# Two head groups in five score units in place of six, in a decoder layer with two attentions

## The chip, the cores and the metric

One core of a Trainium2 chip runs the kernel. The metric is the device time of one execution in microseconds, here 825.18 us as the median of three runs (825.09 to 825.27). Nothing is divided over cores; one core does all four batches.

## What is computed

A pre-norm decoder layer in float32, for 4 batches of 512 rows of 512 numbers, with 16 heads of 32:

```
x = x + self_attention(layernorm(x))        # q, k, v, o projections with biases, causal softmax
x = x + cross_attention(layernorm(x), ctx)  # ctx is both k and v, no projections;
                                            # causal, masked scores are -10000, not -inf
n = layernorm(x)
x = x + relu(n @ W_up.T) @ W_down.T + sum(softmax(top2(n @ W_gate.T))) * (n @ W_expert)
```

In both attentions a softmax over 512 keys is taken for each of 512 queries, 16 heads and 4 batches.

## The kernel before, in words

**Tiling.** The 512 rows of a batch are NT = 4 blocks of P = 128. The 16 heads are NC = 4 groups of HG = 4; one group fills the 128 partitions, a head in 32 of them. Scores are products over the 32 numbers of a head, so four heads' products run as four 32-row tiles of TensorE at once (lines L280 and L370). Values are products of 128 rows with 32 columns, four heads side by side (L429). All the projections are full 128 x 128 products of 512 columns (L221, L233, L638). PSUM is one pool of four `pair`s, each of 128 x 2 x 512 numbers in two banks; everything that TensorE writes takes a pair.

**Two passes over the scores.** An attention first finds the maximum of every row of scores (`maxima`, L267), and then computes the scores again, transposed, subtracts the maxima and takes the exponential (`scores`, L360).

- `maxima(g, blocks)` makes the scores of query blocks of group g against the keys up to the diagonal: blocks (0, 1) together, 128 + 256 = 384 columns, block 2 with 384, block 3 with 512. The four heads fill two pairs. ACT copies each to SBUF (L292, tiles `s`, tags pt0 to pt2 with two buffers each), POOL masks the diagonal (L298), and DVE's jobs reduce each block to its maxima (L310). After block 3 DVE splits the maxima into three bf16 parts (`split`, L323 to L332). `rows(g)` (L334) transposes these parts on TensorE (L338), and a copy makes them the rows `mrow`.
- `scores(g, blocks)` makes the scores of key blocks (0), (1) and (2, 3): 512, 384 and 256 + 128 columns. A bf16 product adds the rows of `mrow` to them (L381). ACT takes the exponentials (L402), POOL zeroes the upper part of the diagonal blocks (L404). `values(g, blocks, pts)` (L416) multiplies with v into the pair `pv`, and with a tile of ones for the denominators. For groups 0 to 2 of the self attention (`added`) the second product is left out: DVE adds the exponentials up over the key blocks (`add_up`, L453, row L458), and four products with ones, in the next group's first values, sum over the partitions (`summed`, L462). `inverse` (L481) transposes denominators and takes reciprocals on DVE; `scale` multiplies on POOL, `divide` on DVE.
- In the cross attention `masked` (L348) and `behind` (L623) add what the fully masked part contributes, since masked scores count as -10000.

**Order.** The order of TensorE, DVE, ACT and POOL is the program's, by hand; only the DMA queue is left to a scheduler. Each engine does its instructions in that order, and waits at its head.

`with_maxima(steps, a, first, norms)` (L780) interleaves the 12 units of an attention's maxima with `fill`: the matmuls of projections or of the feed-forward part of another batch, one of 512 columns at a time (a piece), spread over the units by a cost of their widths. The DVE jobs of one unit run in the fill of the next unit; a norm's job goes with each second unit; so `split(g - 1)` is in the fill of unit (g, blocks (0, 1)), and `rows(g - 1)` come two units later, in the fill of unit (g, block 3); rows(3) is left for the attend. The fill is 36 pieces in batch 0's self attention (`skip` 3 steps were run ahead of it), 34 in batches 1 and 2, 16 in batch 3; for the cross attention 20, 36, 20 and 25.

`attend(a, late)` (L810) runs the 12 units of scores, each followed by the values of the unit two before:

```
for n, (g, j) in enumerate(units):
    waiting.append((g, j, a.scores(g, j)))
    if n == 4:
        for copy in a.rows(late):
            copy(nc.scalar.copy)
    if len(waiting) > 2:
        values()
```

**The start of the cross maxima.** The normed rows of x are transposed (tp_q, L249) in two halves, and ACT copies each half to `cqT` (L257): blocks 0 and 1, then blocks 2 and 3. The first unit of the cross maxima, group 0 and blocks (0, 1), reads the first half only.

Of the kernel before, what the change touches and what calls it, by code (L numbers as in the profile page):

```python
# [18 lines left out]
P = 128  # L19
# [7 lines left out]
def decoder_layer(  # L27
# [232 lines left out]
    class Attention:  # L260
# [6 lines left out]
        def maxima(self, g, blocks):  # L267

            if blocks[0] == 0:
                self.nm[g] = small.tile([P, NT, HG], F32, tag="nm", name=f"nm_{self.name}_{g}")
            first = blocks[0]
            scs = [pair(f"sm_{self.name}_{g}_{first}_{n}") for n in range(2)]
            at = {i: sum((k + 1) * P for k in blocks if k < i) for i in blocks}
            N = sum((i + 1) * P for i in blocks)
            for i in blocks:
                for r in range(HG):
                    h = slice(r * HD, (r + 1) * HD)
                    nc.tensor.matmul(  # L280
                        scs[r // 2][:, r % 2, at[i] : at[i] + (i + 1) * P],
                        lhsT=self.q_t[h, g, i * P : (i + 1) * P],
                        rhs=self.k_t[h, g, : (i + 1) * P],
                        start=(i == first),
                        stop=True,
                        skip_group_check=(i != first),
                    )
            made = []
            for n in range(2):
                W, tag = {0: (S, "pt0"), 2: (N, "pt1"), 3: (S, "pt2")}[first]  # L290
                s = work.tile([P, 2, W], F32, tag=tag, name=f"s_{self.name}_{g}_{first}_{n}")
                nc.scalar.copy(s[:, :, :N], scs[n][:, :, :N])  # L292
                if len(blocks) > 1:

                    diagonal = s.rearrange("p u (k q) -> p (u k) q", k=2)[:, :, :P]
                else:
                    diagonal = s[:, :, N - P : N]
                nc.gpsimd.affine_select(  # L298
                    out=diagonal,
                    in_=diagonal,  # L300
                    compare_op=ALU.is_ge,
                    fill=NEG,
                    base=0,
                    pattern=[[0, 2 * len(blocks)], [-1, P]],
                    channel_multiplier=1,
                )
                made.append(s)

            def largest(n, i):
                nc.vector.tensor_reduce(  # L310
                    self.nm[g][:, i, 2 * n : 2 * n + 2],
                    made[n][:, :, at[i] : at[i] + (i + 1) * P],
                    axis=AX.X,
                    op=ALU.max,
                    negate=True,
                )

            jobs = [(lambda n=n, i=i: largest(n, i)) for n in range(2) for i in blocks]
            if blocks[-1] == NT - 1:
                jobs.append(lambda: self.split(g))  # L320
            return jobs
# [38 lines left out]
        def scores(self, g, blocks):  # L360


            at = {j: sum(S - k * P for k in blocks if k < j) for j in blocks}
            N = sum(S - j * P for j in blocks)
            name = f"{self.name}_{g}_{blocks[0]}"
            scs = [pair(f"sc_{name}_{n}") for n in range(2)]
            for j in blocks:
                for r in range(HG):
                    h = slice(r * HD, (r + 1) * HD)
                    nc.tensor.matmul(  # L370
                        scs[r // 2][:, r % 2, at[j] : at[j] + S - j * P],
                        lhsT=self.k_t[h, g, j * P : (j + 1) * P],
                        rhs=self.q_t[h, g, j * P :],
                        start=(j == blocks[0]),
                        stop=False,
                        skip_group_check=(len(blocks) > 1),
                    )
            for j in blocks:
                for r in range(HG):
                    h = slice(r * HD, (r + 1) * HD)  # L380
                    nc.tensor.matmul(  # L381
                        scs[r // 2][:, r % 2, at[j] : at[j] + S - j * P],
                        lhsT=onesb[h, :],
                        rhs=self.mrow[g][h, j * P :],
                        start=False,
                        stop=True,
                        skip_group_check=(len(blocks) > 1),
                    )
            pts = []
            if blocks[0] == 0 and g in self.added:  # L390

                self.sums[g] = act.tile(
                    [P, 2, 2, S], F32, tag=("ck_t", "beh_t")[g % 2], name=f"sum_{name}"
                )
            for n in range(2):

                W = N if len(blocks) == 1 else S
                if blocks[0] == 0 and g in self.added:
                    pt = self.sums[g][:, n]
                else:  # L400
                    pt = work.tile([P, 2, W], F32, tag=f"pt{blocks[0]}", name=f"pt_{name}_{n}")
                nc.scalar.activation(pt[:, :, :N], scs[n][:, :, :N], AF.Exp)  # L402
                diagonal = pt.rearrange("p u (k q) -> p (u k) q", k=len(blocks))[:, :, :P]
                nc.gpsimd.affine_select(  # L404
                    out=diagonal,
                    in_=diagonal,
                    compare_op=ALU.is_ge,
                    fill=0.0,
                    base=0,
                    pattern=[[0, 2 * len(blocks)], [1, P]],  # L410
                    channel_multiplier=-1,
                )
                pts.append(pt)
            return pts

        def values(self, g, blocks, pts):  # L416
# [3 lines left out]
            first, last = blocks[0] == 0, blocks[-1] == NT - 1  # L420
# [3 lines left out]
            at = {j: sum(S - k * P for k in blocks if k < j) for j in blocks}  # L424
            for u in range(1 if g in self.added else 2):
                for j in blocks:
                    for r in range(HG):
                        h = g * HG + r
                        nc.tensor.matmul(  # L429
                            pv[r * HD : (r + 1) * HD, u, j * P :],  # L430
                            lhsT=ones if u else self.v[:, j, h * HD : (h + 1) * HD],
                            rhs=pts[r // 2][:, r % 2, at[j] : at[j] + S - j * P],
                            start=(j == 0),
                            stop=(j == NT - 1),
                        )
# [5 lines left out]
            if first and g - 2 in self.added:  # L441
                self.scale(g - 2)
            if blocks == (1,) and g - 1 in self.added and g not in self.added:
# [9 lines left out]
        def add_up(self, g, blocks, pts):  # L453
            at = {j: sum(S - k * P for k in blocks if k < j) for j in blocks}
            for n in range(2):
                for j in blocks:
                    to = self.sums[g][:, n, :, j * P :]
                    nc.vector.tensor_tensor(  # L458
                        to, to, pts[n][:, :, at[j] : at[j] + S - j * P], ALU.add
                    )  # L460
# [319 lines left out]
    def with_maxima(steps, a, first=0, norms=()):  # L780
# [6 lines left out]
        units = [(g, i) for g in range(NC) for i in ((0, 1), (2,), (3,))]  # L787
        cost = [sum(k + 1.5 for k in i) for _, i in units]
        done, due, jobs = 0, 0.0, []
        for n, (g, i) in enumerate(units):  # L790
            new = a.maxima(g, i)
            if norms and n % 2 == 0:
                new.append(norms.pop(0))
            due += total * cost[n] / sum(cost)

            for k in range(round(due) - done):
                next(fill, None)
                done += 1
                if k == 1 and i[-1] == NT - 1 and g > 0:
                    jobs = a.rows(g - 1) + jobs  # L800
# [4 lines left out]
        for _ in fill:  # L805
            pass
        run(jobs)
        return NC - 1

    def attend(a, late):  # L810

        units = [(g, j) for g in range(NC) for j in ((0,), (1,), (2, 3))]
        waiting = []

        def values():
            g, j, pts = waiting.pop(0)
            a.values(g, j, pts)
            if g in a.added and j != (2, 3):
                a.add_up(*waiting[0])

        for n, (g, j) in enumerate(units):
            waiting.append((g, j, a.scores(g, j)))
            if n == 4:
                for copy in a.rows(late):
# [3 lines left out]
            if a.cross and j == (0,):  # L828
                behind(a.e, g)
            if a.cross and j == (2, 3):  # L830
                a.masked(g)
# [3 lines left out]
    with tc.manual_schedule(engines=BY_HAND):  # L835
# [7 lines left out]
        skip, between_cross, ahead = 3, [], []  # L843
# [100 lines left out]
```

## Time and profile before

| | us |
|---|---|
| median of three runs | 825.18 |
| the profiled execution | 825.04 |
| its span, first to last instruction | 823.3 |
| self attention, maxima, batch 0 / batch 3 (first score to first score of the attend) | 45.3 / 28.4 |
| self attention, attend, batch 0 | 31.1 |
| cross attention, maxima, batch 0 / batch 1 | 31.8 / 45.3 |
| cross attention, attend, batch 0 | 34.8 |

The stages are read from the timeline of the profiled execution, from the first instruction named to the first of the next stage; those of the maxima hold the fill too. The page gives each engine's busy time and share of the span: PE is TensorE's matmuls, PEld its weight loads, DVE, ACT and POOL the vector, scalar and GpSimd engines. The granted clock of TensorE was 1.00 through the span. The part of the page on the chain follows the work that ended last back from the end; its shares say which engine's work set the time. A group row gives line, engine, operation, output and input shapes and their number, then busy us and the mean in ns of one, then the idle time of that engine ahead of them and what ended it. In a timeline a row has start, duration, engine, line, operation, the number of neighbours put together, and the wait ahead of it in brackets.

### The profile page before, as it was taken

The numbers are of one execution on the slowest core, as the hardware profiler recorded it, in microseconds if no ns is written. First come the engines' busy times: TensorE is split into PE (matmuls) and PEld (weight loads), VectorE is DVE, ScalarE is ACT, GpSimd is POOL, SyncE is SP. The second block draws the span as 40 slices with busy tenths as digits, with TensorE's granted clock in tenths as the row PEclk, the third lists the DMA queues.
The fourth block names the chain that finished last, engine by engine and source line by source line (L and its number), as shares of the span: only waits on it lengthen the run. The fifth ranks groups of instructions, "written<-read, shape, count | busy, mean of one in ns | idle before, by whom it ended". The sixth has DMA issues, their size and how long they took to land.

```text
span 823.3 us, 14456 instructions
## 1 busy us (share of the span) xinstructions
PE 813.3 (99%) x5800; PEld 368.8 (45%) x5800; DVE 544.6 (66%) x937; ACT 398.0 (48%) x502; POOL 298.3 (36%) x549
## 2 busy tenths in 40 slices
PE   8999999999999999999999999999999999999998
PEld 7344454444444454334534445444543444444543
DVE  2578735967678834587868873596779835887512
ACT  2456526762456515556155652676257814565110
POOL 4434512343334732224233471244234643343100
PEclk9999999999999999999999999999999999999999
DMA  9600000001010000030100000000102000000101
GB/s 340 236 27 15 1 1 1 2 2 52 1 39 14 2 1 1 0 103 2 52 14 14 1 2 0 1 2 2 53 3 74 29 1 0 1 2 2 52 0 51
DMA packets 13539, 24.54 MB, mean 30 GB/s; under 512 B 1952, under 2 KB 1952, under 8 KB 13472
## 3 DMA queue, kind: packets, MB, share of 16 engines
q1 hardware_dynamic: 13184, 23.09, 8.3%
q8 instruction: 45, 0.74, 0.4%
q10 hardware_dynamic: 288, 0.52, 0.2%
q14 instruction: 22, 0.18, 0.1%
HBM read 19.42 MB, written 4.19 MB: 29 GB/s over the span
## 4 chain that ended last, share of the span: by engine, by line
PE 94%; DVE 3%; ACT 1%; issue 1%; DMA 0%; POOL 0%; ACTq 0%
PE pm_qk L233 13%; PE pv_c L429 9%; PE pm_d L221 7%; PE pm_u L233 7%; PE pm_v L221 7%; PE pm_o L638 7%; PE pm_e L221 6%; PE pv_s L429 6%; PE sm_c L280 6%; PE sc_s L370 6%; PE sc_c L370 5%; PE sm_s L280 5%; DVE nm_s L310 1%; PE sc_s L381 1%; PE sc_c L381 1%; PE tp_x L666 1%
## 5 line engine op out<-in xcount | busy, mean ns | idle before, releaser
L310 DVE TENSOR_REDUCE nm_c<-s_c 128x2 f32<-128x256 f32 (+3 forms) x128 | 96.3, 810 | 36.6 <-POOL s_c L298 36.6
L310 DVE TENSOR_REDUCE nm_s<-s_s 128x2 f32<-128x256 f32 (+3 forms) x128 | 96.7, 810 | 24.4 <-POOL s_s L298 24.4
L292 ACT COPY s_s<-sm_s 128x768 f32<-128x768 f32 (+1 forms) x96 | 78.8, 874 | 69.0 <-PE sm_s L280 51.2
L292 ACT COPY s_c<-sm_c 128x768 f32<-128x768 f32 (+1 forms) x96 | 78.9, 875 | 48.7 <-PE sm_c L280 34.1
L402 ACT ACTIVATE pt_c<-sc_c 128x768 f32<-128x768 f32 (+1 forms) x96 | 78.5, 884 | 29.3 <-PE sc_c L381 24.8
L298 POOL TENSOR_SCALAR_AFFINE_SELECT s_c<-s_c 128x256 f32<-128x256 f32 (+1 forms) x96 | 46.5, 485 | 118.5 <-ACT s_c L292 117.4
L404 POOL TENSOR_SCALAR_AFFINE_SELECT pt_c<-pt_c 128x256 f32<-128x256 f32 (+1 forms) x96 | 57.4, 605 | 70.5 <-ACT pt_c L402 69.5
L298 POOL TENSOR_SCALAR_AFFINE_SELECT s_s<-s_s 128x256 f32<-128x256 f32 (+1 forms) x96 | 46.6, 488 | 91.4 <-ACT s_s L292 90.6
L458 DVE TENSOR_TENSOR sum_s<-sum_s,pt_s 128x512 f32<-128x512 f32 (+1 forms) x72 | 63.1, 914 | 7.6 <-PE pv_s L429 6.6
L221 PE MATMUL pm_d<-wdown_sb,hT 128*128 128x512 f32 x128 | 61.7, 611 | 0.0
L221 PE MATMUL pm_e<-wexp_sb,fT 128*128 128x512 f32 x128 | 61.2, 608 | 0.4 <-DVE x L760 0.4
L233 PE MATMUL pm_u<-fT,wup_sb 128*128 128x512 f32 x128 | 60.6, 609 | 0.0
L402 ACT ACTIVATE pt_s<-sc_s 128x768 f32<-128x768 f32 (+1 forms) x72 | 55.8, 837 | 9.4 <-PE sc_s L381 7.0
L370 PE MATMUL sc_s<-qT,kT 32*128 32x128 f32 (+3 forms) x512 | 57.4, 466 | 1.9 <-DVE x L760 1.3
L233 PE MATMUL pm_qk<-xnT,wk_sb 128*128 128x512 f32 x120 | 59.3, 612 | 0.0
L221 PE MATMUL pm_v<-wv_sb,xnT 128*128 128x512 f32 x128 | 58.8, 600 | 0.0
L638 PE MATMUL pm_o<-wo_sb,oT_s 128*128 128x512 f32 x128 | 57.8, 596 | 0.0
L233 PE MATMUL pm_qk<-xnT,wq_sb 128*128 128x512 f32 x120 | 57.6, 606 | 0.0
L404 POOL TENSOR_SCALAR_AFFINE_SELECT pt_s<-pt_s 128x256 f32<-128x256 f32 (+1 forms) x72 | 48.4, 676 | 21.4 <-ACT pt_s L402 20.0
L370 PE MATMUL sc_c<-cqT,ckT 32*128 32x128 f32 (+3 forms) x512 | 51.5, 467 | 1.3 <-ACT pt_c L402 1.3
L280 PE MATMUL sm_c<-ckT,cqT 32*128 32x512 f32 (+3 forms) x512 | 49.4, 468 | 0.0
L280 PE MATMUL sm_s<-kT,qT 32*128 32x512 f32 (+3 forms) x512 | 48.1, 467 | 0.0
(148 smaller groups left out, 1183.5 us busy)
## 6 DMA issues: line engine op xcount, KB each, us to landing
cv<-in_ctx_dram SPq DMA_DIRECT2D x16, 256.0 KB, 4.2
out_dram<-x SPq DMA_DIRECT2D x16, 256.0 KB, 2.0
x<-in_x_dram SPq DMA_DIRECT2D x14, 256.0 KB, 4.1
xin<-in_x_dram SPq DMA_DIRECT2D x12, 256.0 KB, 2.6
wq_sb<-in_wq_dram SPq DMA_DIRECT2D x2, 512.0 KB, 6.0
wk_sb<-in_wk_dram SPq DMA_DIRECT2D x2, 512.0 KB, 7.7
wv_sb<-in_wv_dram SPq DMA_DIRECT2D x1, 1024.0 KB, 8.3
wo_sb<-in_wo_dram SPq DMA_DIRECT2D x1, 1024.0 KB, 9.9
```

Of the source, the lines that this page charges most:

```text
L221: nc.tensor.matmul(pm, lhsT=lhs_t[:, c, t * P : (t + 1) * P], rhs=w[:, c, :], start=(c == 0), stop=(c == NC - 1),)
L233: nc.tensor.matmul(pm, lhsT=w[:, c, f * P : (f + 1) * P], rhs=rhs_t[:, c, :], start=(c == 0), stop=(c == NC - 1),)
L280: nc.tensor.matmul(scs[r // 2][:, r % 2, at[i] : at[i] + (i + 1) * P], lhsT=self.q_t[h, g, i * P : (i + 1) * P], rhs=self.k_t[h, g, : (i + ...
L292: nc.scalar.copy(s[:, :, :N], scs[n][:, :, :N])
L298: nc.gpsimd.affine_select(out=diagonal, in_=diagonal, compare_op=ALU.is_ge, fill=NEG, base=0, pattern=[[0, 2 * len(blocks)], [-1, P]], cha ...
L310: nc.vector.tensor_reduce(self.nm[g][:, i, 2 * n : 2 * n + 2], made[n][:, :, at[i] : at[i] + (i + 1) * P], axis=AX.X, op=ALU.max, negate=True,
L370: nc.tensor.matmul(scs[r // 2][:, r % 2, at[j] : at[j] + S - j * P], lhsT=self.k_t[h, g, j * P : (j + 1) * P], rhs=self.q_t[h, g, j * P :] ...
L402: nc.scalar.activation(pt[:, :, :N], scs[n][:, :, :N], AF.Exp)
L404: nc.gpsimd.affine_select(out=diagonal, in_=diagonal, compare_op=ALU.is_ge, fill=0.0, base=0, pattern=[[0, 2 * len(blocks)], [1, P]], chan ...
L429: nc.tensor.matmul(pv[r * HD : (r + 1) * HD, u, j * P :], lhsT=ones if u else self.v[:, j, h * HD : (h + 1) * HD], rhs=pts[r // 2][:, r % ...
L458: nc.vector.tensor_tensor(to, to, pts[n][:, :, at[j] : at[j] + S - j * P], ALU.add)
L638: nc.tensor.matmul(pms[t // 2][:, t % 2, :], lhsT=a.out[:, c, t * P : (t + 1) * P], rhs=wo_sb[:, c, :], start=(c == 0), stop=(c == NC - 1),)
```

## The change

Both passes take two groups of heads in five units of 512 columns in place of six units of 384, 384 and 512:

- maxima of groups g and g + 1: [(g, 2), (g, 0)], [(g+1, 2), (g+1, 0)], [(g, 1), (g+1, 1)], [(g, 3)], [(g+1, 3)], where (g, i) is query block i of group g, widths 384 + 128, 256 + 256 and 512;
- attend: [(g, 0)], [(g, 3), (g, 1)], [(g, 2), (g+1, 2)], [(g+1, 0)], [(g+1, 3), (g+1, 1)], where (g, j) is key block j.

An attention has 10 units of each kind, not 12. Matmuls and their columns stay the same in number. Copies and exponentials are all of 128 x 1024, 80 of each in each kind of attention where there were 96. All of `s` and `pt` share one tag of six buffers of 128 x 2 x 512.

In `with_maxima` the fill is spread evenly; a norm's job goes with every unit; rows(0) and rows(1) come in the fill of units 5 and 6, and rows(2) and rows(3) in the attend, behind the scores of units 1 and 4 (`late`), with their copies on ACT. `skip` is 4, so batch 0's self maxima have 32 pieces of fill.

The unit [(g, 2), (g+1, 2)] ends nothing of group g but its values, and opens the `pv` of group g + 1 by its block 2: two `pv` pairs are alive then. `add_up` of (g+1, 2) is held until the values of (g+1, 0) are issued.

```diff
-            if norms and n % 2 == 0:
+            if norms:
                 new.append(norms.pop(0))
-            due += total * cost[n] / sum(cost)
-
-            for k in range(round(due) - done):
+            due += total / len(units)
+
+            count = round(due) - done
+            for k in range(count):
                 next(fill, None)
                 done += 1
-                if k == 1 and i[-1] == NT - 1 and g > 0:
-                    jobs = a.rows(g - 1) + jobs
+                if k == min(1, count - 1) and n in (5, 6):
+                    jobs = a.rows(n - 5) + jobs
                 run(jobs[:1])
                 jobs = jobs[1:]
...
-        return NC - 1
+        return late
...
-        units = [(g, j) for g in range(NC) for j in ((0,), (1,), (2, 3))]
-        waiting = []
+
+        units = []
+        for g in range(0, NC, 2):
+            units += [[(g, 0)], [(g, 3), (g, 1)], [(g, 2), (g + 1, 2)]]
+            units += [[(g + 1, 0)], [(g + 1, 3), (g + 1, 1)]]
+        waiting, held = [], []
 
         def values():
-            g, j, pts = waiting.pop(0)
-            a.values(g, j, pts)
-            if g in a.added and j != (2, 3):
-                a.add_up(*waiting[0])
-
-        for n, (g, j) in enumerate(units):
-            waiting.append((g, j, a.scores(g, j)))
-            if n == 4:
-                for copy in a.rows(late):
+            made = waiting.pop(0)
+            a.values(made)
+
+            if len(made) > 1 and made[0][1] == 2:
+                held.append(made[1:])
+            elif waiting and waiting[0][0][1] > 0:
+                if made[0][1] == 0 and held:
+                    a.add_up(held.pop())
+                a.add_up(waiting[0] if waiting[0][0][1] == 3 else waiting[0][:1])
+
+        for n, pieces in enumerate(units):
+            waiting.append(a.scores(pieces))
+            if n in late:
+                for copy in a.rows(late[n]):
                     copy(nc.scalar.copy)
             if len(waiting) > 2:
                 values()
-            if a.cross and j == (0,):
-                behind(a.e, g)
-            if a.cross and j == (2, 3):
-                a.masked(g)
+            if a.cross and pieces[0][1] == 0:
+                behind(a.e, pieces[0][0])
+            if a.cross and n % 5 in (2, 4):
+                a.masked(pieces[0][0])
...
-        skip, between_cross, ahead = 3, [], []
+        skip, between_cross, ahead = 4, [], []
```

`maxima`, `scores`, `values` and `add_up` take a list of pieces (g, block), each with its own columns, in place of one group and its blocks; `values` calls a new function `shares(g, blocks)` for each group of the unit:

```diff
+        def values(self, made):
+            for g in sorted({g for g, *_ in made}):
+                self.shares(g, [(j, c, pts) for k, j, c, pts in made if k == g])
+        def shares(self, g, blocks):
+            js = {j for j, *_ in blocks}
+            first = js == {0} if g % 2 == 0 else js == {2}
+            last = js == {2} if g % 2 == 0 else 1 in js
             if first:
                 self.pv[g] = pair(f"pv_{self.name}_{g}")
```

## The prediction

> **What bounds the kernel now.** I read the shares of busy time first, then the chain of waits, then the list of waits, and last the timeline of TensorE around the units that the change touches.
>
> ```profile
> PE 813.3 (99%) x5800; PEld 368.8 (45%) x5800; DVE 544.6 (66%) x937; ACT 398.0 (48%) x502; POOL 298.3 (36%) x549
> PE 94%; DVE 3%; ACT 1%; issue 1%; DMA 0%; POOL 0%; ACTq 0%
> ```
>
> TensorE is the bound nearly everywhere: 99% busy and 94% of the chain, at a granted clock of 1.00. So a microsecond taken from TensorE's queue is a microsecond of the end, unless a wait takes its place. The waits that TensorE has on the other engines are small (the list gives 1.3 us for the cross scores behind the exps, 0.6 us for the self scores), but "busy" hides some: a matmul that is queued behind a wait can count as running. I therefore work from start to start.
>
> **What a unit costs TensorE.** The change removes no matmul and no column; it removes units: two of twelve in each maxima and each attend. What is a unit worth? The timeline of TensorE around one maxima unit (start, duration, instruction, how many):
>
> ```profile
> 23.98 1.45 PE L233 MATMUL pm_qk<-xnT,wk_sb 128*128 128x512 f32 x3
> 25.36 0.93 PE L280 MATMUL sm_s<-kT,qT 32*128 32x384 f32 x8
> 26.22 1.13 PE L233 MATMUL pm_qk<-xnT,wk_sb 128*128 128x512 f32 x2
> 27.18 0.59 PE L233 MATMUL pm_qk<-xnT,wq_sb 128*128 128x512 f32 x1
> ```
>
> An f32 matmul of 512 columns goes through in two passes of 0.43 us, so 384 columns should take 2 x 0.32 = 0.64 us. The unit starts at 25.36 and the next projection at 26.22: 0.86. The two passes of that projection then take 0.96 to the next start where 0.86 is the rule, and the entry costs another 0.09. Together about 0.42 us for going into 32-row tiles and out again, whatever the unit's width. For the attend, one whole group of the cross attention, which has no stall:
>
> ```profile
> 174.65 1.14 PE L370 MATMUL sc_c<-cqT,ckT 32*128 32x512 f32 x8
> 175.62 0.39 PE L381 MATMUL sc_c<-mrow_c,onesb 32*128 32x512 bf16 x4
> 175.94 0.85 PE L429 MATMUL pv_c<-pt_c,cv 128*32 128x384 f32 x8
> 176.61 0.83 PE L429 MATMUL pv_c<-pt_c,ones 128*32 128x384 f32 x8
> 177.37 0.93 PE L370 MATMUL sc_c<-cqT,ckT 32*128 32x384 f32 x8
> ```
>
> Scores of 512 columns: 0.97 from start to start for 0.86 of work (+0.11); mask rows 0.32 for 0.21 (+0.11); values and ones 1.43 for 1.29 (+0.14). So 0.36 us for each unit. Removed: 2 x 8 maxima units x 0.42 = 6.7 us and 2 x 8 attend units x 0.36 = 5.7 us, **12.4 us** in all.
>
> Here a rule speaks against the change. The Trainium skill, "TensorEngine Tiling (Array Packing)", section Instruction Overhead, puts the overhead of tiling at some 60 cycles on each matmul. The number of matmuls stays, so by that rule nothing is gained and only the costs below are left (825.0 + 5.3 = about 830). The rows above put the overhead at the change of tile shape, not at the matmul: inside a shape, eight passes run at width times rate. I go by the rows.
>
> **ACT, POOL, DVE.**
>
> ```profile
> L292 ACT COPY s_s<-sm_s 128x768 f32<-128x768 f32 x64 | 48.0, 803 | 43.1 <-PE sm_s L280 25.3 <-POOL s_s L298 10.9 <-issue 5.8
> L292 ACT COPY s_s<-sm_s 128x1024 f32<-128x1024 f32 x32 | 30.8, 1015 | 25.9 <-PE sm_s L280 25.9
> ```
>
> (Groups apart by shape; 803 and 1015 are mean ns.) 256 more elements cost 212 ns, so 768 elements are 636 ns and the fixed part about 170; back to back, exps step by 0.91 and 0.70, so only 0.06 us of it is exclusive. ACT loses 64 copies and exps and POOL 64 selects, together a few us on engines that are half idle: worth nothing by themselves, since TensorE hides them. What matters is the latency: every evacuation becomes 0.91–1.02 us instead of two in three at 0.70–0.80, and a pair of PSUM banks comes free later.
>
> **Cost 1, the start of the cross maxima.** The first unit becomes query blocks 2 and 0; block 2 lies in the second half of cqT, which is copied last.
>
> ```profile
> 127.01 0.60 PE L249 MATMUL tp_q<-ident,xn_q 128*128 128x128 f32 x4
> 127.54 0.94 PE L280 MATMUL sm_c<-ckT,cqT 32*128 32x128 f32 x16
> 127.65 1.02 ACT L257 ACTIVATE cqT<-tp_q 128x1024 f32<-128x1024 f32 x1 [3.00 <-PE tp_q L249]
> ```
>
> Now the scores start at 127.54, with the copy of the second half still ahead. After the change they wait for its end, 128.67 plus some 0.05: 1.18 us, and all of TensorE's fill is queued behind. Four times: **+4.7 us**, and this one is certain (the order of the instructions shows the wait).
>
> **Cost 2, transposes moved.** rows(2) goes from the fill to the attend's second unit. Four transposes cost there about 0.33 us instead of 0.25 in the fill: 8 x 0.08 = **+0.6**. Its copy stands on ACT, behind it the exps of unit 1.
>
> **Cost 3, the attends.** Without stalls a self group is 1280 columns x (1.68 + 0.42 ns) of scores and mask = 2.69, values 2.15, denominators 0.86 (summed on DVE) or 2.15, and 3 x 0.36: 6.77 us, the last group 8.06. Three and one with 0.33 of transposes make 28.7; the stage takes 31.12 (67.01 to 98.13), so 2.4 us are stalls. The start has 1.05 of it (third unit's scores at 69.47, then 70.39, when the first exps free their pairs; first values at 71.40, 4.39 after the start where 3.34 is the work), and each further group 0.41. After the change all exps are wide and rows(2)'s copy stands among them: I lay out 1.38 for the start, 0.17 at each of five units, 0.39 where the new pv pair of group g+1 is opened while pv of g is alive (two of four pairs held, so scores wait for an exp's end), 0.55 where the denominators of group 2 wait for DVE's late adds. That is 3.2; a stall at one place lets ACT catch up for the next, so I take 2.8 (bounds 2.4 and 3.6). Self attend: 31.12 − 0.72 + 0.33 + 0.4 = 31.1. Cross (34.81 now, 1.0 of stalls): −0.72 + 0.33 + 0.33 at the start + 0.1 = 34.85. So **the attends give their gain back**: the 5.7 us is not seen.
>
> ```profile
> 79.00:85.00 6.00, 6.00 (x72) 2.31 (x65) 4.91 (x6) 4.28 (x6) 3.32 (x5) 1.00 0.01 3
> ```
>
> This row (window; busy us of PE, PEld, DVE, ACT, POOL) shows why ACT does not become the bound in the steady self attend, 4.28 of 6.00. The Trainium skill's same page, section PSUM Bottleneck, warns that once tiling has sped TensorE up the PSUM copy may be the bottleneck. If it were, the stage would be ACT's 20 exps x 0.91 + 2.4 + 1.2 = 21.8 us; it is 31.1. It is the latency and DVE (4.91 of 6.00) that bite.
>
> **Cost 4, transposes one unit after their split.** rows(0) and rows(1) now stand in units 5 and 6, one unit after the units whose jobs hold their split, two before. PE queues the transposes behind DVE's split; everything on TensorE stands behind that. From the end of a block-3 unit to its split I find 6.0–7.2 us in the short cross stages, 7.2–10.0 in the self stage of batch 0, 5.8–9.9 in that of batch 3; the distance to the transposes would be about 7.9 (2 x 3.0 + 1.9), 10.3 and 7.2. So it just fits, with 0.3 us here and there where mrow's copy stands ahead of the next split on DVE. No row shows this wait; bounds 0 and 0.3 on each of 32, 9.6. I take **+1.0**.
>
> **Sum by stage.** Self maxima: two units 0.83 and rows(2) 0.28: −1.1 x 3; in batch 3 DVE is busy 5.5–5.9 of each 6 us, so −0.4 there; −3.7 in all. Cross maxima: −1.1 + 1.18, four times: +0.3. Attends 0.0 and +0.2. Transposes' waits +1.0. Together −2.2: 825.04 (profiled run; its span 823.3 and 1.7 around it) becomes **822.8**. The median of three runs, 825.18, is 0.14 above the profiled one; I leave that out.
>
> **Rivals.** (a) *The attends keep their gain*: exps still end in time, for which the unstalled cross group above speaks and the self group's stall speaks against. Then 825.0 − 12.4 + 4.7 + 0.6 = about 818. (b) *Slower by DVE*: the splits come later than the transposes in each maxima stage. It decides from a lag above some 7.9 us in the short cross stages, where I read 7.2 at most today; a job of norms now in every unit instead of every second, and reduces of one wider unit ahead of the split, push it that way. At its price of 9.6 us, in place of my 1.0: 822.8 + 8.6 = 831; half of it gives 827. (c) *PSUM's four pairs bind in the self attend* (two pv pairs open): 3.6 us of stalls and not 2.8, with 0.3 more at the cross starts: 822.8 + 3.2 + 0.8 = 826.5 at most, about 825, no change.
>
> **Chances.** My sum 0.40, (a) 0.13, (c) 0.20, (b) 0.27. A measurement of this kernel tells about 0.2% (1.65 us) from no change. Faster: two thirds of my sum's case, all of (a), a few of (c): 0.46. Slower: (b) and a few of (c): 0.33. The range goes from (a) to the middle of (b): 817.5 to 829.5; within the likeliest case alone it is 821 to 825.
>
> **What would show it.** Right: the first sm_c of each cross maxima waits about 1.2 us for ACT's cqT; L292 shows 80 copies of s_s and 80 of s_c, all 1024 wide; maxima stages of the self attention 44.2 in batch 0; attends about 31.1 and 34.8. Wrong: self attends near 30.3 (then (a)), PEld of the parts waiting on DVE's L332 by more than 2 us in all (then (b)), scores waiting on exps by more than 1 us in a self attend's later groups (then (c)). The forecast fails too if a unit's 0.42 is not saved when two groups share a unit, since the tile's weights still change with each block.

## The result, and the profile after

The changed kernel takes **833.24 us** (median of four executions, 832.54 to 834.08) against 825.14 for the kernel before: a ratio of 1.0098, 95% interval 1.0085 to 1.0111. It is slower by 8.1 us, where 822.8 was forecast and the range ended at 829.5. The profiled execution took 832.54 with a span of 830.8, 7.5 above before. Two of the four executions lie 1.4 us higher, at a granted clock of 0.998; that clock has a section of its own below.

The lines of the page that answer to those shown of before:

```profile
PE 806.8 (97%) x5800; PEld 378.1 (46%) x5800; DVE 538.4 (65%) x929; ACT 395.6 (48%) x446; POOL 291.4 (35%) x485
PE 89%; DVE 6%; ACT 3%; issue 1%; DMA 0%; POOL 0%; ACTq 0%
```

TensorE's busy time fell by 6.5 us, so its work did shrink; but its share of the chain fell from 94 to 89%, and that of DVE doubled. The program has become one in which TensorE waits. The list of waits of the changed kernel (who waited for whom, us in total, times, longest) has two that weren't there:

```profile
PEld L347 <- DVE parts L341: 14.3, 9, 2.6
PE sm_c L284 <- ACT cqT L257: 4.5, 4, 1.2
```

The first are the transposes of `rows` behind DVE's split. The weight load's wait begins while earlier matmuls are still running, so 14.3 is more than is lost: from one matmul's start to the next, eight of the 32 sets of transposes are late, by 0.38, 1.35, 0.38, 1.34, 1.33, 1.91, 1.00 and 1.55 us, **9.24 us**. (Seven are in the fill. The one of 1.00, which the expectations below take as 0.8, is at the start of batch 3's self attend, where an unhindered step is 0.25 and not 0.43 us.) The second row is the first cross scores' wait for ACT's copy of the second half, four times; here is the one of batch 0:

```profile
128.31 1.15 PE L284 MATMUL sm_c<-ckT,cqT 32*128 32x384 f32 x16 [1.11 <-ACT cqT L257]
```

By stage, the difference to the kernel before in the profiled executions (us; from the first instruction of a stage to the first of the next, four batches added, batch 0's self maxima from the span's start; the cross start is the stage from the out projection to the first cross score; the stages left out differ by nothing):

| kernel | self maxima | self attend | cross start | cross maxima | cross attend | sum |
|---|---|---|---|---|---|---|
| changed | +2.0 | +2.2 | +4.8 | −2.8 | +1.3 | +7.5 |
| rows_later | −2.9 | +3.3 | +4.8 | −1.5 | +1.3 | +5.0 |
| first_half | +1.9 | +2.2 | 0 | −2.7 | +1.3 | +2.7 |
| all_three | −2.9 | +4.8 | 0 | −1.5 | −0.3 | +0.2 |
| gate_last | +0.2 | +4.1 | +4.8 | −3.6 | +2.1 | +7.6 |
| all_four | −2.0 | +6.6 | 0 | −4.0 | +0.6 | +1.3 |
| attend_only | −0.1 | +0.8 | 0 | 0 | −1.6 | −0.9 |
| maxima_only | −2.8 | +2.9 | 0 | −1.5 | +3.7 | +2.4 |
| before_early_rows | +5.7 | −0.6 | 0 | +3.4 | 0 | +8.5 |
| mixed | −2.5 | +2.0 | 0 | −4.0 | −0.6 | −5.1 |

The profiled executions of rows_later, all_three, maxima_only and before_early_rows hold, in batch 3, one stretch of lower clock each, worth some 1.6 us (told at the end); their medians, given below, count it only as often as it came.

Within the changed kernel's first cell, batch 0 gained 1.0, batches 1 and 2 lost 0.4 each and batch 3 lost 2.2. The self maxima of batch 0 and the cross maxima of batches 0 to 2, which have no late transposes or one of 0.38, gained what was forecast for them, 1.0 to 1.1 each.

### The profile page after: what moved, and what is told of

Its sections match the earlier page's. It is cut to its first block, busy times and chain, and to the rows that moved or that the text cites. A ratio compares the mean times of both kernels' runs of the same rounds, so it can differ in the third digit from the quotient of the medians.

```text
span 830.8 us, 14267 instructions
## 1 busy us (share of the span) xinstructions
PE 806.8 (97%) x5800; PEld 378.1 (46%) x5800; DVE 538.4 (65%) x929; ACT 395.6 (48%) x446; POOL 291.4 (35%) x485
## 4 chain that ended last, share of the span: by engine, by line
PE 89%; DVE 6%; ACT 3%; issue 1%; DMA 0%; POOL 0%; ACTq 0%
PE pm_qk L233 13%; PE pv_c L451 9%; PE pm_u L233 7%; PE pm_v L221 7%; PE pm_o L661 7%; PE pm_e L221 6%; PE pv_s L451 6%; PE pm_d L221 5%; PE sc_s L381 5%; PE sc_c L381 5%; PE sm_c L284 5%; PE sm_s L284 4%; DVE nm_s L315 2%; PE sc_s L392 1%; PE sc_c L392 1%
## 5 line engine op out<-in xcount | busy, mean ns | idle before, releaser
L315 DVE TENSOR_REDUCE nm_c<-s_c 128x2 f32<-128x768 f32 (+3 forms) x128 | 96.1, 810 | 42.9 <-POOL s_c L303 42.9
L315 DVE TENSOR_REDUCE nm_s<-s_s 128x2 f32<-128x768 f32 (+3 forms) x128 | 96.3, 810 | 28.6 <-POOL s_s L303 28.6
L295 ACT COPY s_s<-sm_s 128x1024 f32<-128x1024 f32 x80 | 77.1, 1015 | 69.6 <-PE sm_s L284 41.6
L295 ACT COPY s_c<-sm_c 128x1024 f32<-128x1024 f32 x80 | 77.1, 1015 | 51.9 <-PE sm_c L284 27.7
L412 ACT ACTIVATE pt_c<-sc_c 128x1024 f32<-128x1024 f32 x80 | 77.1, 1023 | 33.9 <-PE sc_c L392 28.6
L420 POOL TENSOR_SCALAR_AFFINE_SELECT pt_c<-pt_c 128x512 f32<-128x512 f32 (+1 forms) x80 | 56.1, 708 | 71.7 <-ACT pt_c L412 71.2
L481 DVE TENSOR_TENSOR sum_s<-sum_s,pt_s 128x256 f32<-128x256 f32 (+2 forms) x72 | 60.8, 909 | 15.8 <-PE pv_s L451 15.8
L412 ACT ACTIVATE pt_s<-sc_s 128x1024 f32<-128x1024 f32 x56 | 54.3, 1023 | 11.2 <-PE sc_s L392 5.7
L420 POOL TENSOR_SCALAR_AFFINE_SELECT pt_s<-pt_s 128x512 f32<-128x512 f32 (+1 forms) x56 | 48.5, 875 | 16.5 <-ACT pt_s L412 15.7
L381 PE MATMUL sc_c<-cqT,ckT 32*128 32x384 f32 (+3 forms) x512 | 50.7, 462 | 2.0 <-ACT pt_c L412 2.0
```

Source lines behind the costliest of these rows:

```text
L295: nc.scalar.copy(s, scs[n])
L315: nc.vector.tensor_reduce(self.nm[g][:, i, 2 * n : 2 * n + 2], made[n][:, :, c : c + (i + 1) * P], axis=AX.X, op=ALU.max, negate=True,)
L381: nc.tensor.matmul(scs[r // 2][:, r % 2, c : c + S - j * P], lhsT=self.k_t[h, g, j * P : (j + 1) * P], rhs=self.q_t[h, g, j * P :], start= ...
L412: nc.scalar.activation(pt, scs[n], AF.Exp)
L420: nc.gpsimd.affine_select(out=diagonal, in_=diagonal, compare_op=ALU.is_ge, fill=0.0, base=0, pattern=[[0, 2], [0, len(pieces)], [1, P]], ...
L481: nc.vector.tensor_tensor(to, to, pts[n][:, :, c : c + S - j * P], ALU.add)
```

## Where the split is late

The worst place in batches 0 to 2 is rows(1) in the self maxima of batches 1 and 2. TensorE's and then DVE's timeline there (start, duration, instruction, the wait ahead of it in brackets):

```profile
238.24 1.98 PE L221 MATMUL pm_d<-wdown_sb,hT 128*128 128x512 f32 x4
241.40 0.40 PE L347 MATMUL mt_s<-identb,parts 128*128 128x128 bf16 x4 [1.19 <-DVE parts L341]
```

```profile
235.17 0.39 DVE L752 MAX8 top<-lg 128x8 f32<-128x8 f32 x4 [3.61 <-PE lg L743]
...
236.98 1.21 DVE L315 TENSOR_REDUCE nm_s<-s_s 128x2 f32<-128x1024 f32 x1
238.10 0.42 DVE L353 COPY mrow_s<-mt_s 128x512 bf16<-128x512 bf16 x1
238.44 1.21 DVE L315 TENSOR_REDUCE nm_s<-s_s 128x2 f32<-128x1024 f32 x1
...
241.12 0.23 DVE L341 TENSOR_TENSOR parts<-rest_s,parts 128x16 bf16<-128x16 f32 x1
```

DVE is not busy ahead of this: it stands idle for 3.61 us at the head of its queue, because the gate's MAX8 waits for the gate's matmuls (lg), which TensorE reaches only after the next unit. Behind it the two reduces of group 1's block 3 wait, and between them the copy of mrow of group 0. The unit of block 3 was over at 230.2; its split ends at 241.35, 11.1 us later, and TensorE stands at the transposes from about 240. The prediction read this lag in the short cross stages and in the self stages of batches 0 and 3, whose fills hold no gate. In the kernel before it was already 10.25 us at this place: the unit of block 3 was over at 230.44, and the split and its transposes were

```profile
240.47 0.23 DVE L332 TENSOR_TENSOR parts<-rest_s,parts 128x16 bf16<-128x16 f32 x1
242.83 0.39 PE L338 MATMUL mt_s<-identb,parts 128*128 128x128 bf16 x4
```

so 2.1 us were to spare there, with two units between.

## The experiments

**rows_later: the transposes two units after their split.**

```diff
-                if k == min(1, count - 1) and n in (5, 6):
-                    jobs = a.rows(n - 5) + jobs
+                if k == min(1, count - 1) and n in (6, 7):
+                    jobs = a.rows(n - 6) + jobs
```

> The changed kernel with rows(0) and rows(1) one unit later (units 6 and 7, so two units after their splits, as in the kernel before); everything else as changed. Theory A, TensorE waits at these transposes for DVE's split: the seven waits in the fill that I read in the changed kernel's timeline (0.38, 1.35, 0.38, 1.34, 1.33, 1.91 and 1.55 us from start to start) go, 8.2 us: 833.2 becomes about 825, with the cross start (4.7) and the attends as they are. Rival B, DVE is late as a whole, so the wait comes back at the next thing that needs it (the buffers of s, or the attend's first scores behind mrow): over 830. In the timeline A has no L347 weight load behind L341 in the fill.

Measured: 829.96 us (828.74 to 830.34), ratio 1.0055 (1.0040 to 1.0070) to before. No weight load of `rows` in the fill waits for the split any more. The same place as above, in this kernel:

```profile
237.45 1.99 PE L221 MATMUL pm_d<-wdown_sb,hT 128*128 128x512 f32 x4
239.27 0.39 PE L347 MATMUL mt_s<-identb,parts 128*128 128x128 bf16 x4
239.49 1.94 PE L221 MATMUL pm_d<-wdown_sb,hT 128*128 128x512 f32 x4
```

So A is right in kind, and the maxima of batches 1 and 2 become 1.1 us shorter each, those of batch 3's self attention 2.5. But the end comes 3.3 earlier, not 8.2 (3.8 between the executions at the highest clock, 832.54 and 828.74). Batch 3 shows where the rest is: its self attend is 1.1 us longer than in the changed kernel, its cross maxima 2.0 (of which some 1.6 is a lower clock behind a wait, told at the end). In batch 3 B holds: the wait for DVE comes back at the next thing that needs it.

**first_half: the cross maxima begin with blocks 1.**

```diff
-            units += [[(g, 2), (g, 0)], [(g + 1, 2), (g + 1, 0)], [(g, 1), (g + 1, 1)]]
+            two = [[(g, 2), (g, 0)], [(g + 1, 2), (g + 1, 0)]]
+            one = [[(g, 1), (g + 1, 1)]]
+            units += one + two if a.cross and g == 0 else two + one
```

> The changed kernel with the first three maxima units of the cross attention's groups 0 and 1 in another order: [(0, 1), (1, 1)] first, which reads only the first half of cqT, then the two units with block 2. Theory A: the wait of the first cross scores for the second copy of cqT goes, 1.19 us four times: 833.2 - 4.7 = 828.5. Rival B: the wait is only moved to the second unit, or TensorE is late there anyway: 832 or more.

Measured: 828.46 us (827.73 to 829.31), ratio 1.0039 (1.0024 to 1.0054), 4.8 us under the changed kernel. The cross start is exactly as before in all four batches, and no other stage moves by more than 0.12. Theory A.

**all_three: both, and rows(2) behind the attend's fourth scores** (`late = {3: 2, 4: NC - 1}` in place of `{1: 2, 4: NC - 1}`).

> The changed kernel with rows(0) and rows(1) one unit later, the cross attention's units begun with [(0, 1), (1, 1)], and rows(2) behind the attend's fourth scores in place of its second. If the three costs are separate: 833.2 - 8.2 (waits for splits) - 4.7 (cross start) - 0.8 (rows(2)'s wait for its split in batch 3) - about 0.4 x 8 (its PSUM pair and its wait for an exp at the start of the attend, if that is what the start lost) = 816 to 819.5, faster than the kernel before. If DVE or ACT is the bound and the waits only change their place: 825 or more.

Measured: 823.87 us (823.62 to 825.57, twelve executions), ratio 0.9990 (0.9981 to 0.9998). Faster than before by a hair, and 4 to 8 us short of what the sum of separate costs gave. The cross attends gain from the later rows(2): −0.07 each where the changed kernel had +0.32. The self attends lose (+0.83 for +0.61). And batch 3 keeps its losses: +2.3 in the self attend, +2.5 in the cross maxima, here:

```profile
710.29 0.70 PE L284 MATMUL sm_c<-ckT,cqT 32*128 32x256 f32 x4
712.52 1.54 PE L284 MATMUL sm_c<-ckT,cqT 32*128 32x256 f32 x12 [1.53 <-DVE x L773]
713.99 3.22 PE L221 MATMUL pm_d<-wdown_sb,hT 128*128 128x512 f32 x4
```

The second half of a unit's scores needs a PSUM pair which DVE's addition of pm_d to x frees; that addition stands in DVE's queue behind nine reduces and two splits, at which DVE has worked without a pause since 700.3. With the transposes out of the way TensorE waits here instead. Some 1.6 of the 2.5 is a lower clock behind this wait, told at the end.

**gate_last and all_four: the gate behind the down projections**, in the changed kernel and in all_three (the first of three lines that change alike).

```diff
-                between_self, between_cross = gates[:1] + ups + gates[1:] + downs, experts
+                between_self, between_cross = gates[:1] + ups + downs + gates[1:], experts
```

> The changed kernel with one step of the fill moved: the gate (eight small matmuls to lg and its chain on DVE and ACT) goes behind the down projections in place of ahead of them. Theory A: the waits for split(1) in the self maxima of batches 1 and 2 (1.35 and 1.34 us) and for split(0) in the cross maxima of batch 3 (1.55) come from this chain, which stands ahead of the reduces in DVE's queue and waits for lg; they go: 833.2 - 4.2 = 829.0. Rival B: the wider units and a norm in every unit make DVE late: 832 or more.

> all_three with the gate behind the down projections. In all_three the cross maxima of batch 3 were 2.5 us longer than in the kernel before, since TensorE waited for a PSUM pair that DVE's addition of pm_d frees late. If the gate's chain makes DVE late there: 823.9 - 2.5 = 821.4, and nothing of the lower clock behind that wait. If DVE is late in that stage by its load alone: 823 to 824.

Measured: gate_last 832.73 us (832.41 to 835.39), ratio 1.0100 (1.0082 to 1.0117); all_four 826.34 (826.06 to 826.56), ratio 1.0013 (1.0006 to 1.0020). Neither is what I expected; gate_last lands at rival B's number, but not for its reason. In gate_last the waits for split(1) in batches 1 and 2 and for split(0) in batch 3's cross maxima are gone, and those stages are 1.0, 1.0 and 0.9 us shorter than in the changed kernel: the chain of the gate was what made the split late. But the attends behind them are 1.0, 1.0 and 0.9 us longer, since the same chain now stands ahead of split(2) and rows(2) waits for it at the attend's start. In the self attend of batch 1 (TensorE):

```profile
257.17 1.14 PE L381 MATMUL sc_s<-qT,kT 32*128 32x128 f32 x12 [0.46 <-DVE top L752]
257.93 0.59 PE L392 MATMUL sc_s<-mrow_s,onesb 32*128 32x128 bf16 x8
259.36 0.40 PE L347 MATMUL mt_s<-identb,parts 128*128 128x128 bf16 x4 [0.83 <-DVE parts L341]
```

Neither of the two places that were tried for the chain, ahead of the down projections and behind them, is free.

**before_early_rows: the moved transposes alone, in the kernel before.**

```diff
-            for k in range(round(due) - done):
+            count = round(due) - done
+            for k in range(count):
...
-                if k == 1 and i[-1] == NT - 1 and g > 0:
+                if k == min(1, count - 1) and i == (2,) and g > 0:
```

> The kernel before (six units for two groups) with one thing done: rows(g - 1) in the fill of unit (g, block 2) in place of (g, block 3), so one unit after their split. Theory A, what counts is the distance to the split: the slack that the transposes had (1.1 to 7.7 us) shrinks by a unit's 2.4 to 3.9 us, which leaves waits of 1.6 us in batches 1 and 2 of the self attention, about 1.2 twice in batch 3, and little elsewhere: 829 to 832. Rival B, the wait comes from the wider units and the norms in every unit: under 827.

Measured: 832.68 us (832.58 to 833.56), ratio 1.0090 (1.0073 to 1.0106). Without any five-unit form, moving the transposes to one unit behind their split costs as much as the whole change did; but here three sets move in each maxima, where the change moved two, and only a part of the loss is the wait for the split. Waits at the transposes are read in the self stages of all batches (0.63, 0.69, 0.69 and 1.95 us) and once in the cross stage of batch 1 (0.69); the self maxima of batch 3 lost 3.8, the lower clock told at the end among it. The short cross stages lost 1.2 each for another reason. There the transposes now stand directly ahead of the scores of block 3. First the kernel before, then this one, in batch 0:

```profile
140.13 1.14 PE L280 MATMUL sm_c<-ckT,cqT 32*128 32x512 f32 x8
141.20 1.98 PE L233 MATMUL pm_qk<-xnT,wk_sb 128*128 128x512 f32 x4
```

```profile
140.68 0.39 PE L338 MATMUL mt_c<-identb,parts 128*128 128x128 bf16 x4
140.99 1.50 PE L280 MATMUL sm_c<-ckT,cqT 32*128 32x512 f32 x8
142.43 1.98 PE L233 MATMUL pm_qk<-xnT,wk_sb 128*128 128x512 f32 x4
```

The scores take 1.44 us from start to start where they took 1.07. The transposes have taken a PSUM pair that ACT's first copy of block 2 freed, and the second half of the scores starts only when ACT's second copy has ended (141.33). The three places of the stage lose 0.37, 0.48 and 0.36 us, the whole of the 1.2.

**attend_only and maxima_only: half the change each.** attend_only is the kernel before with `scores`, `values`, `add_up` and `attend` of the change, and six-unit maxima; maxima_only has the maxima of all_three and the attend of before, with `late = {3: 2, 5: NC - 1}`, which puts rows(2) behind the fourth scores and rows(3) behind the sixth.

> The kernel before with the change's attend alone (five units; six buffers of one tag for all); the maxima in six units, rows(2) in the fill, rows(3) behind the fifth scores. If rows(2), its product and its PSUM pair ate the gain of the attends: each self attend at 31.0 or less, each cross attend at 34.4, the kernel 825.1 - 0.1 x 4 - 0.4 x 4 = 823. If the wide exps' latency and the two open pv pairs ate it: self 31.5, cross 34.8, the kernel 827.

> The change's maxima in five units with rows(0) and rows(1) one unit later and the cross start of the first half, and the attend of the kernel before in six units, with rows(2) behind its fourth and rows(3) behind its sixth scores. The maxima stages of all_three were 4.2 us shorter than before in sum (with 2.5 lost in batch 3's cross stage); rows(2) costs 8 x 0.33 in the attends: 825.1 - 4.2 + 2.6 = 823.5. If the attends lose more than rows(2)'s own time to it: 825 or more.

Measured: attend_only 824.43 us (824.14 to 824.68), ratio 0.9991 (0.9984 to 0.9998), a gain of 0.7; maxima_only 827.47 (825.80 to 829.37), ratio 1.0025 (1.0014 to 1.0036). Each cross attend in five units is 34.41, 0.40 under before, as the first expectation has it; the self attends of batches 0 to 2 are 31.13, 0.08 over, between the expectation's two figures and nearer the first; batch 3's lost 0.5. In the changed kernel they stand at 35.12 and 31.66. So rows(2) behind the second scores costs 0.71 in a cross attend and 0.53 in a self attend; behind the fourth it costs the cross attend 0.33, which is just the transposes' own time. The difference of 0.38 is the PSUM pair that they take at the start: the changed kernel's cross attend begins

```profile
160.21 1.39 PE L381 MATMUL sc_c<-cqT,ckT 32*128 32x128 f32 x16
161.22 0.59 PE L392 MATMUL sc_c<-mrow_c,onesb 32*128 32x128 bf16 x8
161.75 0.40 PE L347 MATMUL mt_c<-identb,parts 128*128 128x128 bf16 x4
162.46 0.70 PE L381 MATMUL sc_c<-cqT,ckT 32*128 32x256 f32 x4 [0.31 <-ACT pt_c L412]
163.37 0.92 PE L381 MATMUL sc_c<-cqT,ckT 32*128 32x256 f32 x10 [0.21 <-ACT pt_c L412]
```

Two units hold all four pairs; the transposes take the first that an exp frees, so the third unit's halves wait for the second and third exps, 0.91 us apart, in place of the first and second. In all_three, whose stage begins at 157.58, they come 2.51 and 3.42 us after its start, here 3.43 and 4.34:

```profile
160.09 0.70 PE L381 MATMUL sc_c<-cqT,ckT 32*128 32x256 f32 x4
161.00 0.92 PE L381 MATMUL sc_c<-cqT,ckT 32*128 32x256 f32 x10 [0.21 <-ACT pt_c L412]
```

In maxima_only the attend of before pays 0.92 in each cross attend for rows(2) and for rows(3) one unit later: it has no room for them either.

**before_noadd and attend_noadd: are the self attends held by DVE?** `add_up` is left out in the kernel before and in attend_only, so their denominators are incomplete; only the time is read.

> The kernel before without add_up: the 72 additions on DVE that sum the exponentials over the key blocks of groups 0 to 2 in the self attention are left out (those denominators then hold the first key block alone). It is the base for attend_noadd. If DVE's adds hold TensorE in the self attend of the kernel before, that stage falls from 31.05 to below 30.5; if only the latency of the exps does, it stays near 31.0.

> attend_only without the same 72 additions. The attend in five units gained 0.40 us in each cross attention, but lost 0.08 in each self attention. If the difference of 0.5 is DVE's adds (the denominators of group 2 wait for them at the end), the self attend of this kernel is 0.4 us below that of before_noadd. If it is the latency of the exps and selects behind the two open pv pairs, it is no more than 0.1 below, as with the adds.

One execution each (826.16 and 819.45 us). The self attend of batch 0 in both, window and busy us of PE, PEld, DVE, ACT and POOL; first before_noadd, then attend_noadd:

```profile
67.44:98.67 31.23, 31.02 (x382) 14.05 (x381) 10.32 (x17) 21.57 (x28) 14.62 (x27) 1.00 0.01 2
```

```profile
67.33:97.20 29.87, 29.45 (x381) 13.53 (x380) 10.74 (x17) 21.10 (x24) 13.58 (x22) 1.00 0.01 2
```

In the six-unit form the additions cost TensorE nothing (31.05 with them, 31.23 without). In five units they cost 1.26 us (31.13 and 29.87): the five-unit self attend is 1.36 us shorter than the six-unit one without the additions, and the additions, with the waits for them, take all of that back. Why before_noadd is slower with less to do (0.18 in each self attend, 0.43 ahead of batch 0's) is open.

**mixed: five units where they gain.** The maxima of batches 0 to 2 as in all_three; their self attends in five units with rows(2) behind the second scores; every cross attend in five units (rows(2) behind the fourth, and in the fill for batch 3); batch 3's maxima and self attend in six units as in the kernel before. The new lines of the order:

```diff
+            late = (with_maxima if more else with_maxima_six)(between_self, sa, skip, norms)
...
+            (attend if more else attend_six)(sa, late)
...
+            late = (with_maxima if more else with_maxima_six)(steps[3:], ca)
...
+        late = {3 if a.cross else 1: 2, 4: NC - 1}
```

> Five units where the runs so far showed a gain: the maxima of batches 0 to 2 with rows(0) and rows(1) one unit later and the cross start from the first half, their self attend in five units with rows(2) behind the second scores, every cross attend in five units with rows(2) behind the fourth; batch 3's maxima and its self attend in six units as before. Sum of the stage differences measured so far: self maxima -1.0, -0.7, -0.7, 0; self attends +0.6 x 3, 0; cross maxima -1.44, -1.11, -1.44, 0; cross attends -0.07 x 3, -0.4; in all -5.2: 825.2 becomes 820.0. If DVE's lateness is only moved on to the next stage again: 822 or more.

Measured: **820.20 us** (819.89 to 820.22), ratio 0.9940 (0.9926 to 0.9953). It beats both kernels, and the stage differences add to −5.1 where −5.2 was expected. TensorE is back at

```profile
PE 94%; DVE 3%; ACT 1%; issue 1%; DMA 0%; POOL 0%; ACTq 0%
```

## Why the prediction was wrong

- **A unit's worth: right in size.** In rows_later, where no transposes of the fill wait, the six maxima stages of batches 0 to 2 became 1.1 us shorter on average, as forecast (two units, and rows(2) moved out); single ones range from 0.70 to 1.44, and what spreads them is open. 0.36 us for an attend unit: two are 0.72, of which attend_only shows 0.40 in the cross attend; it fits with the 0.3 us that the start was forecast to lose, but that loss was not measured by itself. The 60 cycles on each matmul (the Trainium skill, "TensorEngine Tiling (Array Packing)", Instruction Overhead), which the prediction set against this, are not the whole cost: the matmuls stayed at 5800 and these stages became shorter.
- **Cost 1, the cross start: right.** 4.7 forecast, 4.77 measured, and 4.8 back in first_half.
- **Cost 4, the transposes' waits: this is the step that failed.** "So it just fits" and +1.0 us: they cost 9.24 at the transposes in the changed kernel, at eight places with 0.4 to 1.9 us each. The distances were right (forecast 7.9, 10.3 and 7.2 us; without their waits 8.0 in the short cross stages, 9.8 in the self stages of batches 1 and 2, 7.1 in that of batch 3). The lag of the split was not: for the late sets it is 8.35 in the short cross stages, 11.1 in self batches 1 and 2, 8.4 and 10.4 in self batch 3, 9.3 in batch 3's cross maxima. Three things were missed. The prediction's own 5.8–9.9 for batch 3 does not fit into its 7.2: in the kernel before, the lags there are 5.7 for rows(0) and 8.0 for rows(1). The stages with the gate in their fill were not read, and rows(1) of self batches 1 and 2 stood at 10.25 already. And today's lags were taken for tomorrow's, though the change grew them, most in batch 3 (5.7 to 8.4 and 8.0 to 10.4 in the self maxima, 5.7 to 9.3 in the cross). Which part of the change does that there was not taken apart. That the waits come from the short distance is what rows_later shows: with one unit more no set of the fill waits, and the end comes 3.3 us earlier; the rest of the 8.2 comes back in batch 3.
- **Its bound held by luck.** 9.6 is 0.3 us at each of 32 sets; only 16 are rows(0) and rows(1), and the waits are few and long, not many and short.
- **Cost 3, the attends: too small by 3.3 us** (+0.2 forecast, +3.5 measured; 1.0 of it is the transposes' wait in batch 3). The stage before was taken as 31.12, where the trace has 31.05. 31.1 was forecast for a self attend and 31.66 measured in batches 0 to 2, 34.85 and 35.12 for a cross attend. The sum used 2.8 of a self attend's stalls inside a range of 2.4 to 3.6; measured they are 3.35 (31.66 less the work, 28.7 − 0.72 + 0.33). Moved transposes cost 0.53 to 0.71 there where their own time is 0.33. That DVE bites in the steady self attend was said; that its additions eat the whole gain is what attend_noadd shows.
- **Batch 3's self maxima: the sum's −0.4 is near without the waits** (−0.30 in rows_later), but DVE's lateness then comes out in the attend.
- **The rivals.** (b) was the one that came, at 831 forecast for its full price, but not in its place: it was to decide in the short cross stages, which wait 0.38 each. The long waits are in the stages with the gate in their fill (1.35, 1.34, 1.55) and in batch 3's self attention, which has the least fill (1.33, 1.91, 1.00). (a) is ruled out by the attends. (c) has a part: the transposes' PSUM pair at the attend's start.

The sum with what the runs measured, by stage. Maxima: −6.7 for the units, −2.2 for rows(2) that left them (8 x 0.28) and +8.2 for the waits in the fill make −0.7; measured −0.8. Cross starts: +4.8. Attends: −5.7 for the units, +2.6 for rows(2) (8 x 0.33) and +1.0 for its wait in batch 3 make −2.1; measured +3.5. So what is left, about 5.6 us, lies in the attends: 1.0 in each self attend of batches 0 to 2 (0.8 of it stands in attend_only too, and goes without the additions) and 0.7 in each cross attend (0.3 in attend_only, 0.4 the PSUM pair).

## What to carry to other kernels

A unit that is made wider saves what is paid at its edges, and that saving can be read from start to start in the timeline; but fewer units also shorten, counted in units, the distance between a producer on another engine and its consumer in an in-order queue. For every instruction that moves nearer to its producer, read the slack that it has today, each instance by itself, and subtract the length of a unit: what comes out negative is a stall. It finds a part of them only. Here it gives 1.5, 1.5 and 1.0 us (slack 2.1, 2.1 and 1.3, units of 3.7, 3.7 and 2.4) at places where 1.35, 1.34 and 1.91 came; the other waits of the fill came where the reckoning still left slack, since the producer became later too. Taking one such stall away shows in the end time only if no other wait stands behind it; in batch 3 here the wait took another name.

## What was not expected of the hardware

After a wait of TensorE in the middle of the dense part the granted clock fell. Windows of all_three around the wait at 710 us (us, PE, PEld, DVE, ACT and POOL busy, then the granted clock):

```profile
709.00:712.50 3.50, 1.99 (x11) 0.77 (x9) 3.36 (x8) 0.27 (x1) 0.70 (x2) 1.00 0.00 0
712.50:717.00 4.50, 4.48 (x16) 2.06 (x17) 2.67 (x5) 1.93 (x2) 1.27 (x2) 0.62 0.00 0
717.00:724.00 7.00, 7.00 (x31) 2.57 (x29) 6.52 (x10) 3.85 (x4) 1.68 (x4) 1.00 0.01 2
```

1.90 us passed between two matmuls' starts; then passes of 512 columns took 0.76 to 1.01 us where 0.43 is the rule, for some 3 us, and the stretch cost some 1.6 (the four passes of pm_d 3.06 from start to start where 1.82 is the rule, the scores ahead of them 0.4). It is not in every execution of a kernel: those of all_three fall into two groups, eight about 823.8 (clock 0.999 or 1.000 in seven of them) and four about 825.4 (0.997 or 0.998), and in the changed kernel two of four were 1.4 higher. rows_later and maxima_only show it behind a pause of 1.90 at the same place, and before_early_rows behind 2.38 us at 626.9, with a pass of 1.01. But a pause alone does not decide: the profiled execution of the changed kernel has one of 2.34 us up to 626.9 and keeps a clock of 1.00, and all_three has an earlier one of 1.92 with no drop. The Trainium skill, "TensorE: Matmul & The Clock Gate", Part 1, has the clock fall to half after an idle window of some 3.4 us; half is what the passes show (0.85 for 0.43), but here the drop came behind pauses of 1.9 to 2.4 us, in some executions only. What decides it these runs don't show. A stall of TensorE can thus cost more than its own length.
